# Graph convolutions' sums by row gathers in place of a stored adjacency

## The chip, the cores and the metric

The kernel runs on one core of a Trainium2 chip. The metric is the device time of one execution in microseconds (us); lower is better. The engines are named as in the profile: PE multiplies matrices (PEld is its weight load), DVE is the vector engine, ACT the scalar engine, POOL is GpSimd, and SP only issues DMAs. DMAs can be issued by SP, by ACT or by POOL; those whose rows are addressed by an index in memory (DMA_INDIRECT in the profile) are issued by POOL.

## The reference

There are N = 2500 nodes with D = 256 features, and E = 40000 edges sorted by their destination. The input passes through two blocks; each adds a graph convolution and a mixer to `x`, and then a set of expert networks.

```python
xn = _layernorm(x)
x = x + sage(xn, src, dst) + linear_mix(xn)      # mean over the neighbours, @ W_l.T, + xn @ W_r.T
x = x + top2_of_8_experts(_layernorm(x))
xn = _layernorm(x)
x = x + gcn(xn, src, dst) + transformer(xn)      # transformer: 4 layers, linear attention, FFN of 1024
x = x + experts(x)                               # gelu(x@W1), argmax gate of 8, prob * (H@Wd[e] + bd[e])
```

The change is in `gcn`, two graph convolutions with symmetric norms, where every node is also its own neighbour:

```python
src, dst = concat([src, loops]), concat([dst, loops])
deg = segment_sum(ones, dst); dis = rsqrt(deg)
norm = dis[src] * dis[dst]
h = segment_sum((x @ W1)[src] * norm[:, None], dst) + b1
h = where(h >= 0, h, alpha * h)
h = segment_sum((h @ W2)[src] * norm[:, None], dst) + b2
```

## The kernel before

The 2500 nodes stand as 20 tiles of P = 125 rows (NT = 20), in five groups of four tiles (NG = 5, GT = 4, GC = 500 columns). The code is a straight list of engine instructions: a scheduler orders each engine's queue and puts in the semaphores, so on one engine an instruction that waits holds back all that stand behind it. Work is interleaved by Python generators and by `between` callbacks, which set the order within an engine.

**First stage (0 to about 340 us).** The edge list becomes an adjacency matrix. `build_tile` makes one-hot rows of source and destination, multiplies them on PE (L722), and ACT copies the counts into a bf16 tile `edges` (L725), one group of 500 destinations at a time, each with all 20 source tiles. `neighbours` (L284; its matmul is L292) sums the neighbours' rows as matmuls: for each source tile three bf16 terms of the fp32 table times the counts, in two halves of the features. Its `between` builds the next group's `edges` and moves on the gating of the last group. Then `aT<-pa` copies (L750) take the sums from PSUM, two adds put the products into `X` (L762, L763), and the group's gating scatters its rows, sorted by expert, to `sorted` in DRAM (L407, on POOL). For the second block's use, identity is added to the diagonal blocks (L753) and each group's `edges` is stored as `adj` in DRAM, 12.5 MB in all.

**Second block (628 to about 1815 us).** `first_norm` normalizes the rows and calls `conv_in` for each group: `xn @ W1` times `dis`, kept as three bf16 terms in `table` (`split3`, ACT and POOL) and stored as `tab1` for a general path. `attention(l)` runs the four transformer layers; within one, `ffn` (L1148) works through the groups. `conv_1(g)`, the first convolution of a group, reads that group's `adj` back in pieces and calls `neighbours` again (`pa<-piece,table`); groups 0 and 1 run in layer 0, then one in each layer:

```python
            for g in range(NG):
                if max(g - 1, 0) == l:
                    conv_1(g)
```

It multiplies by `dis` along the columns (`along_rows`), adds b1, applies the two-sided ReLU with `alpha`, multiplies by W2 (`conv_in` again) and stores the terms as `terms2`. `conv_2()` stands behind the fourth layer: it loads `terms2`, calls `neighbours` for five groups (`mm<-piece,table`), turns the sums and adds them, times `dval`, to `X` (L972). GpSimd has two large adds in `ffn`: b2 into `Y` (L1151) and, in the last layer, `Y` into `X` (L1171), and it issues the loads of `b2` and `gm` at the start of each layer (L1029, L1031).

**Last stage.** From 1815 us the gates sort the rows by expert, and from 1960 us the experts work on blocks of 128 rows, each gathered by its index (L1345, POOL) and scattered to the output (L1403, POOL).

A general path, in a loop that runs only if the fast path's tables do not hold the edges (`lost`), follows each block.

Of the kernel before, what the change touches and what calls it, by code (L numbers as in the profile page):

```python
# [9 lines left out]
F32 = mybir.dt.float32  # L10
I32 = mybir.dt.int32
# [5 lines left out]
N = 2500  # L17
# [15 lines left out]
KC = 2  # L33
# [17 lines left out]
def gps_kernel(ctx: ExitStack, tc: tile.TileContext, a, out):  # L51
# [69 lines left out]
    ones = const.tile([P, 128], F32, name="ones")  # L121
    V.memset(ones, 1.0)
# [11 lines left out]
    adj = dram.tile([NG, P, NT, GC], BF16, name="adj")  # L134
    kth = scan.tile([128, 128], BF16, name="kth")
    G.iota(kth, pattern=[[1, 128]], base=0, channel_multiplier=0, allow_small_or_imprecise_dtypes=True)
    identb = scan.tile([P, P], BF16, name="identb")
    V.tensor_copy(identb, ident[:P, :P])
# [24 lines left out]
    begin = probe.tile([P, NQ], I32, name="begin")  # L163
# [47 lines left out]
    cnt = const.tile([P, NT], F32, name="cnt")  # L211

    def count_edges(pool):
# [15 lines left out]
        counts = dram.tile([N], F32, name="counts")  # L229
        nc.sync.dma_start(counts.rearrange("(q m n) -> m q n", q=NQ, n=BD), per)  # L230
        byrow = pool.tile([NT, P], F32, name="byrow")
        nc.sync.dma_start(byrow, counts.rearrange("(i p) -> i p", p=P))
        pc = psum2.tile([P, NT], F32, tag="cx", name="pc")
        T.transpose(pc, byrow, ident[:NT, :NT])
        V.tensor_copy(cnt, pc)
        return lost

    def gather_sums(pool, acc, table):
# [6 lines left out]
        gh = pool.tile([128, CH], F32, name="gh")  # L245
        V.tensor_scalar(gh, ge[:, :, 1], 1.0 / P, -0.496, ALU.mult, ALU.add)
        V.tensor_scalar(gh, gh, MAGIC, -MAGIC, ALU.add, ALU.add)
        gf = pool.tile([128, CH], F32, name="gf")
        V.tensor_copy(gf, ge[:, :, 1])
        V.scalar_tensor_tensor(gf, gh, -float(P), gf, ALU.mult, ALU.add)  # L250
        gs = pool.tile([128, CH], I32, name="gs")
        V.scalar_tensor_tensor(gs, gf, float(NT), gh, ALU.mult, ALU.add)
# [20 lines left out]
    def along_rows(pool, v, g):  # L273

        ps = psum2.tile([128, GC], F32, tag="ag", name="ps")
        for k in range(GT):
            dg = pool.tile([P, P], F32, tag="dg", name="dg")
            V.tensor_scalar(dg, ident[:P, :P], v[:, g * GT + k:g * GT + k + 1], None, ALU.mult)
            T.matmul(ps[:, k * P:(k + 1) * P], ones, dg, start=True, stop=True)
        row = pool.tile([128, GC], F32, tag="row", name="row")  # L280
        S.copy(row, ps)
        return row

    def neighbours(g, table, piece, between=None, banks=None):  # L284


        pa = banks or [psum2.tile([128, GC], F32, tag="ag", name=f"pa{c}") for c in range(2)]
        for k in range(NT):
            e = piece(k)
            for c in range(2):  # L290
                for n in range(3):
                    T.matmul(pa[c], table[:, k, n, c * 128:(c + 1) * 128], e,  # L292
                             start=(k == 0 and n == 0), stop=(k == NT - 1 and n == 2))
            if between is not None:
                between(k)
        return pa
# [238 lines left out]

    sorted1 = adj.rearrange("g p k d -> (g p k d)").bitcast(F32)[0:NE // 2 * N * RW].rearrange("(r c) -> r c", c=RW)
# [75 lines left out]
    with tc.tile_pool(name="lay0", bufs=1) as lay0:  # L612
# [91 lines left out]
        degrees(cnt)  # L704
# [5 lines left out]
        with tc.tile_pool(name="build", bufs=1) as build:  # L710
# [15 lines left out]

            ahead = new_edges()
            for k in range(GT):
                build_tile(ahead, 0, k)
            for g in range(NG):  # L730
                edges = ahead
                for lo, hi in ((0, g * GT), ((g + 1) * GT, NT)):
                    if hi > lo:
                        move(nc.sync, adj[g][:, lo:hi, :], edges[:, lo:hi, :])
# [5 lines left out]
                def between(k):  # L740

                    if k % GT == 1 and k < GT * GT and g + 1 < NG:
                        build_tile(ahead, g + 1, k // GT)
                    if gating is not None and k in (7, 15):
                        next(gating)

                pa = neighbours(g, xb, lambda k: edges[:, k, :], between)
# [3 lines left out]
                for k in range(GT):  # L751
                    o = edges[:, g * GT + k, k * P:(k + 1) * P]
                    V.tensor_tensor(o, o, identb, ALU.add)  # L753
                move(nc.sync, adj[g][:, g * GT:(g + 1) * GT, :], edges[:, g * GT:(g + 1) * GT, :])
# [23 lines left out]
    with tc.tile_pool(name="lost0", bufs=1) as pool, tc.For_i(0, n_lost, 1):  # L778
# [8 lines left out]
        nc.sync.dma_start(tab0.rearrange("(p k) d -> p k d", p=P), acc[:, :, :D])  # L787
# [78 lines left out]
    with tc.tile_pool(name="big", bufs=4) as big, tc.tile_pool(name="hid", bufs=8) as hid, \  # L866
# [30 lines left out]
        tab1 = dram.tile([N, D], F32, name="tab1")  # L897
        terms2 = dram.tile([NG, P, GT, 3, D], BF16, name="terms2")
        table = conv.tile([P, NT, 3, D], BF16, name="table")
        dval = const.tile([P, NT], F32, name="dval")  # L900
        V.tensor_scalar(dval, dis, valid, None, ALU.mult)

        def conv_in(g, src, w, keep):

            for b in range(0, GT, 2):
                i = g * GT + b
                if keep and b:
                    t = conv.tile([P, 3, D], F32, tag="t3", name="t3")[:, 0:2, :]
                else:
                    t = conv.tile([P, 2, D], F32, tag="t", name="t")  # L910
                ps = psum2.tile([P, 2, D], F32, tag="ag", name="ps")
                for k in range(2):
                    for c in range(2):
                        T.matmul(ps[:, k, :], src[:, c, (b + k) * P:(b + k + 1) * P], w[:, c, :], start=(c == 0), stop=(c == 1))
                V.tensor_tensor(t, ps, dis[:, i:i + 2, None].to_broadcast([P, 2, D]), ALU.mult)
                if keep:
                    move(nc.sync, tab1.rearrange("(p k) d -> p k d", p=P)[:, i:i + 2, :], t)
                    split3(table[:, i:i + 2], t, G)
                else:
                    t3 = conv.tile([P, 2, 3, D], BF16, tag="t3", name="t3")  # L920
                    split3(t3, t, G)
                    move(nc.sync, terms2[g][:, b:b + 2], t3)

        def conv_1(g):


            def piece(k):
                if k % KC == 0:
                    piece.tile = conv.tile([P, KC, GC], BF16, tag="piece", name="piece", bufs=4)
                    move(nc.sync, piece.tile, adj[g][:, k:k + KC, :])  # L930
                return piece.tile[:, k % KC, :]

            row = along_rows(conv, dis, g)
            pa = neighbours(g, table, piece)
            u = conv.tile([128, 2, GC], F32, tag="u", name="u")
            for c in range(2):
                V.tensor_tensor(u[:, c, :], pa[c], row, ALU.mult)
            for c in range(2):
                neg = conv.tile([128, GC], F32, tag="row", name="neg")
                V.tensor_scalar(neg, u[:, c, :], bcol[:, 0, c:c + 1], 0.0, ALU.add, ALU.min)  # L940
                S.activation(u[:, c, :], u[:, c, :], AF.Relu, bias=bcol[:, 0, c:c + 1])
                V.scalar_tensor_tensor(u[:, c, :], neg, alpha, u[:, c, :], ALU.mult, ALU.add)
            conv_in(g, u, wc2, False)

        def conv_2():

            for g in range(NG):
                move(nc.sync, table[:, g * GT:(g + 1) * GT], terms2[g])
            u = big_T()

            def sums(g):
                def piece(k):
                    if k % KC == 0:
                        piece.tile = hid.tile([128, GC], F32, tag="h", name="piece")[:P].bitcast(BF16).rearrange(
# [534 lines left out]
```

## Time and profile before

| | us |
|---|---|
| median of three runs | 2159.9 (2159.02 to 2162.81) |
| the profiled execution | 2163.04 |
| its span | 2161.2, mean granted PE clock 0.96 |

The stages of the profiled execution, from its busy time in stretches:

| stretch, us | what runs | PE busy | DVE busy | POOL busy |
|---|---|---|---|---|
| 0 to 340 | edges, first convolution, gating | 252.5 | 207.1 | 87.0 |
| 340 to 570 | first experts | 186.2 | 74.5 | 47.6 |
| 570 to 628 | `first_norm` | 50.1 | 42.5 | 18.4 |
| 628 to 1678 | four layers and `conv_1` | 1044.5 | 447.6 | 89.6 |
| 1678 to 1815 | `conv_2` | 133.2 | 27.0 | 2.5 |
| 1815 to 1960 | gates and sorting | 122.6 | 31.5 | 23.9 |
| 1960 to 2161 | experts | 170.9 | 65.9 | 46.5 |

The page's slices show how evenly PE is filled, and the clock it was granted, each digit a tenth in a slice of 54 us:

```profile
PE   2699973999689999999999999999999998995996
...
POOL 2302322222130201001010010000211000122222
PEclk9799986999799999999999999999999999997999
```

A row of groups in the profile reads: line, engine, operation, written tile `<-` read tiles, shapes, count, then busy time and mean ns of one, then the idle time of the engine just before and what ended it. A row that answers for one line gives the least, median and greatest duration in ns, and the first and last start.

### The profile page before, as it was taken

The numbers are of one execution on the slowest core, as the hardware profiler recorded it, in microseconds if no ns is written. First come the engines' busy times: TensorE is split into PE (matmuls) and PEld (weight loads), VectorE is DVE, ScalarE is ACT, GpSimd is POOL, SyncE is SP. The second block draws the span as 40 slices with busy tenths as digits, with TensorE's granted clock in tenths as the row PEclk, the third lists the DMA queues.
The fourth block names the chain that finished last, engine by engine and source line by source line (L and its number), as shares of the span: only waits on it lengthen the run. The fifth ranks groups of instructions, "written<-read, shape, count | busy, mean of one in ns | idle before, by whom it ended". The sixth has DMA issues, their size and how long they took to land. (4 is left out here: it accounts for less than half of the span.)

```text
span 2161.2 us, 25307 instructions
## 1 busy us (share of the span) xinstructions
PE 1959.8 (91%) x9035; PEld 1309.3 (61%) x9035; DVE 896.2 (41%) x2822; ACT 580.8 (27%) x989; POOL 315.6 (15%) x288
## 2 busy tenths in 40 slices
PE   2699973999689999999999999999999998995996
PEld 2556643887466577676676767666676443334665
DVE  6866542333644346435463443635441023212333
ACT  1433201222361222223323133232322000331220
POOL 2302322222130201001010010000211000122222
PEclk9799986999799999999999999999999999997999
DMA  4022445665512200111001100022100435111100
GB/s 121 9 81 71 110 144 165 200 198 175 139 39 66 70 6 13 35 43 38 0 13 42 50 24 0 13 63 77 29 0 1 126 95 183 36 28 33 33 19 24
DMA packets 83119, 141.30 MB, mean 65 GB/s; under 512 B 18700, under 2 KB 64254, under 8 KB 82227
## 3 DMA queue, kind: packets, MB, share of 16 engines
q1 hardware_dynamic: 66193, 112.35, 17.7%
q0 software_dynamic: 13840, 20.89, 3.5%
q10 hardware_dynamic: 2949, 6.33, 1.1%
q8 instruction: 76, 1.25, 0.2%
q14 instruction: 61, 0.49, 0.1%
HBM read 103.85 MB, written 37.61 MB: 65 GB/s over the span
## 5 line engine op out<-in xcount | busy, mean ns | idle before, releaser
L1166 PE MATMUL mm<-w,h 128*125 128x256 f32 x1280 | 286.1, 379 | 0.0
L1156 PE MATMUL mm<-xT,w 128*128 128x500 f32 x640 | 282.9, 582 | 0.0
L1166 PEld LDWEIGHTS mm<-w,h 128*125 128x125 f32 x1280 | 239.2, 188 | 43.0 <-issue 9.2
L292 PEld LDWEIGHTS <-table 125*128 125x128 bf16 x1200 | 117.1, 98 | 126.7 <-issue 1.7
L1156 PEld LDWEIGHTS mm<-xT,w 128*128 128x128 f32 x640 | 119.0, 190 | 109.2 <-issue 100.8
L1159 ACT ACTIVATE h<-mm,bf 128x500 f32<-128x500 f32 x160 | 107.6, 677 | 216.6 <-PE mm L1156 216.5
L1151 POOL TENSOR_TENSOR tok<-tok,b 125x1024 f32<-125x1024 f32 x20 | 47.3, 2364 | 684.5 <-DVE tok L1143 632.4
L292 PE MATMUL pa<-piece,table 125*128 125x500 bf16 x600 | 138.1, 374 | 0.0
L292 PE MATMUL pa<-edges,xb 125*128 125x500 bf16 x600 | 134.4, 377 | 1.7 <-ACT edges L725 1.7
L292 PE MATMUL mm<-piece,table 125*128 125x500 bf16 x600 | 127.3, 374 | 0.0
L1167 DVE TENSOR_TENSOR tok<-tok,mm 125x256 f32<-125x256 f32 x80 | 33.5, 419 | 206.8 <-PE mm L1166 178.7
L1394 PE MATMUL py<-wd,taken 128*128 x432 | 96.9, 381 | 10.0 <-DVE taken L1384 10.0
L828 PE MATMUL mm<-xc,wt 128*128 128x128 f32 x752 | 97.1, 283 | 7.6 <-DVE idx L834 4.0
L828 PEld LDWEIGHTS mm<-xc,wt 128*128 128x128 f32 x752 | 89.6, 194 | 18.0 <-DVE xc L824 12.9
L292 PEld LDWEIGHTS <-xb 125*128 125x128 bf16 x600 | 58.2, 100 | 64.0 <-issue 4.1
L842 PE MATMUL py<-w,h 128*128 x376 | 96.1, 382 | 0.9 <-ACT h L832 0.9
L1394 PEld LDWEIGHTS py<-wd,taken 128*128 128x128 f32 x432 | 81.2, 190 | 25.3 <-DVE taken L1384 13.1
L832 ACT ACTIVATE h<-mm,wt 128x128 f32<-128x128 f32 x188 | 53.8, 369 | 137.6 <-issue 127.3
L357 ACT ACTIVATE xT<-mm,mixc 128x500 f32<-128x500 f32 x80 | 58.9, 768 | 116.1 <-PE mm L352 82.0
L725 ACT CAST edges<-mm 125x500 bf16<-125x500 f32 x100 | 64.7, 784 | 89.4 <-PE mm L722 80.3
L1254 PE MATMUL mm<-xTf,w 128*128 128x500 f32 x160 | 79.2, 618 | 6.0 <-DMA w<-in_L_ffn_W_dram 6.0
L1067 PE MATMUL mm<-xT,wa 128*128 128x500 f32 x160 | 76.4, 622 | 3.9 <-ACT xT L357 3.9
(363 smaller groups left out, 2833.6 us busy)
## 6 DMA issues: line engine op xcount, KB each, us to landing
wt<-in_expert_in_dram SPq DMA_DIRECT2D x47, 514.0 KB
piece<-adj SPq DMA_DIRECT2D x100, 218.8 KB
w<-in_L_mix_W_dram SPq DMA_DIRECT2D x8, 1024.0 KB
wd<-in_L_ffn_Wd_dram SPq DMA_DIRECT2D x8, 1024.0 KB
xs<-sorted SPq DMA_DIRECT2D x47, 130.0 KB
w<-in_L_ffn_W_dram SPq DMA_DIRECT2D x8, 512.0 KB
adj<-edges SPq DMA_DIRECT2D x2, 1750.0 KB
terms<-t SPq DMA_DIRECT2D x10, 336.0 KB
```

Source lines behind the costliest of these rows:

```text
L292: T.matmul(pa[c], table[:, k, n, c * 128:(c + 1) * 128], e, start=(k == 0 and n == 0), stop=(k == NT - 1 and n == 2))
L357: S.activation(o, ps, AF.Identity, bias=shift[:, c:c + 1], scale=gain[:, c:c + 1])
L725: S.copy(o.rearrange("p s (n d) -> p n s d", d=BD), ps[:P].rearrange("p (n s d) -> p n s d", n=BD, d=BD))
L828: T.matmul(ps[:, j * TS:(j + 1) * TS], wt[:, c * F0 + j * 128:c * F0 + (j + 1) * 128], xc[:, c * TS:(c + 1) * TS], start=(c == 0), stop=(c ...
L832: S.activation(h[:, j * TS:(j + 1) * TS], ps[:, j * TS:(j + 1) * TS], AF.Gelu, bias=wt[:, 2 * F0 + j:2 * F0 + j + 1])
L842: T.matmul(ps, h[:, j * TS:(j + 1) * TS], w2[:, ds(e, 1), j, :], start=(j == 0), stop=(j == NJ - 1))
L1067: T.matmul(ps, wk[:, kc, c * 128:(c + 1) * 128], hT[:, kc, g * GC:(g + 1) * GC], start=(kc == 0), stop=(kc == 1))
L1156: T.matmul(ps, w1[:, c, j * 128:(j + 1) * 128], fT[:, c, g * GC:(g + 1) * GC], start=(c == 0), stop=(c == 1))
L1159: S.activation(h, ps, AF.Gelu, bias=bf[:, l, j:j + 1])
L1166: T.matmul(ps, hh[j][:, k * P:(k + 1) * P], w2[:, j, :], start=(j == 0), stop=(j == nj - 1))
L1254: T.matmul(ps, w1[:, c, j * 128:(j + 1) * 128], xT[:, c, g * GC:(g + 1) * GC], start=(c == 0), stop=(c == 1))
L1394: T.matmul(ps, h[:, j * TS:(j + 1) * TS], wd[:, ds(e, 1), j, :], start=(j == 0), stop=(j == nj - 1))
```

## The change

The adjacency is built for the first block only and no longer stored. In its place each node gets a rank by its number of edges (`rank_nodes`): a one-hot of the count in 64 bins, running sums by ten matmuls, and a record of 16 bytes (node, first edge, `dis`) scattered to its rank in `byrank`. That table is read back as 20 columns of 128 ranks; for each, one gather fetches a window of as many edges as the list `MOST` allows its ranks, and edges that belong to another node are replaced by row N, a row of zeros. The steps of `rank_nodes` run within the first stage, from `between` of groups 1 to 4.

A convolution is then, for each of the 20 columns of ranks, one gather of the nodes' own rows and up to 42 of neighbours' rows, each of 128 rows of 1 KB, four to a tile, summed by DVE. The first convolution's sums get b1 and the ReLU in rank order and are scattered to `tab2`; the second's are scattered to `sums2`, and `conv_out` multiplies by `dval` and W2 and adds to `X` behind the last layer. `conv_step` puts the sums' DVE instructions at places within the layers, by a calendar of constants. `sorted1`, which used the memory of `adj`, has its own tile and is filled with zeros in the first stage.

Besides that, the `b2` and `gm` loads go from POOL's queue to ACT's, the two GpSimd adds go to DVE, tables in DRAM are laid out by node, and the general path gets a flag of its own (`lost1`).

```diff
+MOST = (42, 24, 22, 21, 20, 19, 18, 18, 17, 16, 16, 15, 15, 14, 14, 13, 13, 12, 11, 9)
+SUM = 4
+LEAD = 5
+GATHER = 1.27
+LANDING = 12.0
+LAYER = 237.0
+AHEAD = 40.0
+NBIN = 64
...
+    def rank_nodes(pool):
...
+        for i in range(NT):
+            made.append(G.indirect_dma_start(
+                out=byrank, out_offset=bass.IndirectOffsetOnAxis(ap=at[:, i:i + 1], axis=0), in_=rec[:, i, :], in_offset=None,
+            ))
...
+        yield
+        byr = pool.tile([128, NT, 4], F32, name="byr")
+        nc.gpsimd.dma_start(byr, byrank.rearrange("(j p) c -> p j c", p=128))
...
+        yield
+        wins = pool.tile([128, heads_of[NT], 2], I32, name="wins")
+        hit = pool.tile([128, heads_of[NT]], F32, name="hit")
+        for j in range(NT):
+            part = slice(heads_of[j], heads_of[j + 1])
+            G.indirect_dma_start(
+                out=wins[:, part, :].rearrange("p e t -> p (e t)"), out_offset=None, in_=pairs,
+                in_offset=bass.IndirectOffsetOnAxis(ap=from_[:, j:j + 1], axis=0),
+            )
+            V.tensor_scalar(hit[:, part], wins[:, part, 0], byr[:, j, 0:1], None, ALU.is_equal)
+        yield
...
+            for n in range(0, 80, 16):
+                nc.sync.dma_start(sorted1.rearrange("(p r) c -> p r c", p=P)[:, n:n + 16, :],
+                                  nothing[:, None, :].to_broadcast([P, 16, RW]))
...
-                        move(nc.sync, adj[g][:, lo:hi, :], edges[:, lo:hi, :])
...
+                    if g > 0 and k in (3, 11, 19):
+                        next(ranking, None)
...
-                for k in range(GT):
-                    o = edges[:, g * GT + k, k * P:(k + 1) * P]
-                    V.tensor_tensor(o, o, identb, ALU.add)
-                move(nc.sync, adj[g][:, g * GT:(g + 1) * GT, :], edges[:, g * GT:(g + 1) * GT, :])
...
-        def conv_1(g):
...
-        def conv_2():
...
+        def gathers(tab, finish):
...
+            steps = [(j, k) for j in range(NT) for k in range(0, MOST[j] + 1, SUM)]
+            pieces = {}
...
+            def fetch(n):
+                j, k = steps[n]
+                t = conv.tile([128, SUM, D], F32, tag="piece" if k else "total", name="piece", bufs=LEAD + 1 if k else 3)
+                m = min(SUM, MOST[j] + 1 - k)
+                for i in range(m):
+                    by = node[:, j:j + 1] if k + i == 0 else nbr[:, heads_of[j] + k + i - 1:heads_of[j] + k + i]
+                    G.indirect_dma_start(out=t[:, i, :], out_offset=None, in_=tab,
+                                         in_offset=bass.IndirectOffsetOnAxis(ap=by, axis=0))
+                pieces[n] = t, m
...
+            for n in range(LEAD):
+                fetch(n)
+            for n, (j, k) in enumerate(steps):
+                yield GATHER * (sum(min(SUM, MOST[i] + 1 - b) for i, b in steps[:n + 1]) + j)
+                t, m = pieces.pop(n)
+                if k == 0:
+                    total = t
                 else:
...
+                    V.tensor_tensor(total[:, :m, :], total[:, :m, :], t[:, :m, :], ALU.add)
+                if n + LEAD < len(steps):
+                    fetch(n + LEAD)
+                if k + SUM > MOST[j]:
+                    V.tensor_tensor(total[:, 0:2, :], total[:, 0:2, :], total[:, 2:4, :], ALU.add)
+                    sums = conv.tile([128, D], F32, tag="sums", name="sums", bufs=3)
+                    V.tensor_tensor(sums, total[:, 0, :], total[:, 1, :], ALU.add)
+                    finish(j, sums)
...
+        def between(j, o):
...
+            b = conv.tile([128, D], F32, tag="b", name="b")
+            S.activation(b, b1row, AF.Identity, scale=disr[:, 0, j:j + 1])
+            V.scalar_tensor_tensor(o, o, disr[:, 1, j:j + 1], b, ALU.mult, ALU.add)
+            neg = conv.tile([128, D], F32, tag="neg", name="neg")
+            V.tensor_scalar(neg, o, 0.0, alpha, ALU.min, ALU.mult)
+            V.scalar_tensor_tensor(o, o, 0.0, neg, ALU.max, ALU.add)
...
+            to_nodes(tabs[1], j, o)
...
+        def conv_step(now):
+            while under and under[0][1] + under[0][2] + LANDING <= now:
+                run, _, begun = under.pop(0)
+                with tc.issue_after(last["add"]):
+                    passed = next(run, None)
+                if passed is not None:
+                    under.insert(0, (run, passed, begun))
+                elif begun == 0:
+                    run = gathers(tabs[1], lambda j, o: to_nodes(sums2, j, o))
+                    under.append((run, next(run), now))
...
+        def conv_out(g, rows, turned):
...
+            s = rows[:, g * GT:(g + 1) * GT, :]
+            move(nc.gpsimd, s, by_node(sums2)[:, g * GT:(g + 1) * GT, :])
+            V.tensor_tensor(s, s, dval[:, g * GT:(g + 1) * GT, None].to_broadcast([P, GT, D]), ALU.mult)
+            sT = turned[:, :, g * GC:(g + 1) * GC]
+            transpose_group(turned, g, lambda k: s[:, k, :])
...
-                nc.gpsimd.dma_start(b2, row_bcast(a["L1_mix_b2"], l * D, D, 128))
+                nc.scalar.dma_start(b2, row_bcast(a["L1_mix_b2"], l * D, D, 128))
...
+                conv_step(LAYER * l + AHEAD * i / NT * 0.7)
...
-                G.tensor_tensor(o, o, b2[:P, None, :].to_broadcast([P, GT, D]), ALU.add)
+                V.tensor_tensor(o, o, b2[:P, None, :].to_broadcast([P, GT, D]), ALU.add)
...
+                def beside(step):
+                    conv_step(LAYER * l + AHEAD + (LAYER - 1.6 * AHEAD) * (g + step / (nj + GT)) / NG)
...
-            for g in range(NG):
-                if max(g - 1, 0) == l:
-                    conv_1(g)
...
-        conv_2()
+        with tc.issue_after(last["product"]), tc.issue_after(last["add"]):
+            conv_step(1e9)
+            rows, turned = big_tok(), big_T()
+            for g in range(NG):
+                conv_out(g, rows, turned)
```

## The prediction

> **What bounds the kernel now.** I read the page's forty slices first, then the costliest groups, then a table of busy time by stage.
>
> ```profile
> PE 1959.8 (91%) x9035; PEld 1309.3 (61%) x9035; DVE 896.2 (41%) x2822; ACT 580.8 (27%) x989; POOL 315.6 (15%) x288
> ...
> L1151 POOL TENSOR_TENSOR tok<-tok,b 125x1024 f32<-125x1024 f32 x20 | 47.3, 2364 | 684.5 <-DVE tok L1143 632.4
> L292 PE MATMUL pa<-piece,table 125*128 125x500 bf16 x600 | 138.1, 374 | 0.0
> ...
> L292 PE MATMUL mm<-piece,table 125*128 125x500 bf16 x600 | 127.3, 374 | 0.0
> ```
>
> PE is the bound and POOL nearly idle. The two L292 groups are the graph convolutions. By stage (columns: window, length, busy us of PE, PEld, DVE, ACT, POOL, PE clock, DMA share, GB/s):
>
> ```profile
> 300.00:340.00 40.00, 11.85 (x53) 9.92 (x51) 14.55 (x60) 1.52 (x2) 16.47 (x16) 0.60 0.74 214
> ...
> 628.00:897.00 269.00, 265.99 (x1141) 180.99 (x1142) 114.43 (x359) 69.34 (x106) 27.49 (x20) 1.00 0.13 35
> 897.00:1156.00 259.00, 258.11 (x1084) 177.28 (x1083) 117.84 (x385) 78.41 (x115) 18.18 (x12) 1.00 0.10 27
> 1156.00:1417.00 261.00, 260.11 (x1094) 178.96 (x1093) 117.87 (x385) 78.41 (x115) 18.19 (x12) 1.00 0.10 27
> 1417.00:1678.00 261.00, 260.12 (x1093) 178.77 (x1091) 97.49 (x282) 78.41 (x115) 25.77 (x13) 1.00 0.12 33
> 1678.00:1815.00 137.00, 133.15 (x649) 64.19 (x648) 27.02 (x102) 3.46 (x6) 2.51 (x2) 0.99 0.35 97
> ```
>
> Rows two to five are the four transformer layers, PE over 98% busy; the last is the second convolution with nothing beside it. In the timeline its last `X` add ends at 1811.6 and the gates' first matmul (L1254) starts at 1819.5, after 6.0 us on its weights. Without convolution a layer needs about 229 us of PE (259 less 28.3 of L292 and about 2 of its small products; the first 209).
>
> **What goes.** All of both L292 groups: some 30 us in each of three layers, 60 in the first, and the 137 us stage. The stored adjacency (12.5 MB) and its readings go too, but the new zero-fill of `sorted1` writes 10.4 MB in the same stage, so I count nothing for bandwidth. GpSimd's 25 large adds move to VectorE. The bound then passes to POOL.
>
> **What comes: gathers.** The sum of `MOST` is 349, plus 20 own rows: 369 gathers (the short description says 367) and 20 scatters per convolution, 778 POOL instructions for two. The nearest row is the expert stage's gather of 128 rows of 1040 bytes; this rate is the forecast's main term.
>
> ```profile
> L1345 POOL DMA_INDIRECT X<-adj,whence x20: 945/956/1131, 1965.7 to 2066.2; - x20
> ```
>
> In the timeline one follows another after 0.30 us of issue, so the period is 1.26 us (1967.06, 1968.33, 1969.58). A gather lands 2.9 us after its start. 389 × 1.26 = **490 us per convolution**, 980 for both: more than the four layers' PE work of 209 + 3 × 229 = 896. DMA itself is no limit: four gathers in 1965 to 1990 took 7.9% of the sixteen engines over 25 us, 0.5 us each.
>
> **A rule that speaks against it.** The Trainium skill's page "SBUF — State Buffer", box "The 'DVE blocks DMA' trap", says that while VectorE runs a two-port operation (an fp32 copy in SBUF), GpSimd is locked out and cannot write its DMA's descriptors: 620 ns became about 3100. Its section "Who interferes with whom" exempts a tensor_tensor, thus the new adds, but not tensor_scalar. The trace has POOL DMAs beside such operations (start, length, engine; "x2" is two operations in one row):
>
> ```profile
> 1969.58 0.95 POOL L1345 DMA_INDIRECT X<-adj,whence  x1 [0.30 <-issue]
> 1969.58 0.74 DVE L1357 TENSOR_SCALAR xh<-X 128x256 f32<-128x256 f32 x2 [3.07 <-DMA X<-adj,whence]
> ...
> 2145.59 0.69 DVE L1384 COPY taken<-hs 128x1024 f32 x1
> 2145.62 1.50 POOL L1403 DMA_INDIRECT out_dram<-yo,idx  x1 [4.02 <-DVE yo L1402]
> ```
>
> The scatter took 1.50 in place of 0.97, 0.53 more: something like the lock is there. But of nine gathers that had 0.41 us tensor_scalars beside them, as the first, eight took 0.95 and one 1.13: +0.02 on average. In the layers there are 140 such tensor_scalars (L1143, L365). By the trace's worst case or the rule's "blocked until the VectorE operation ends" that is 140 × 0.5 = +70 us; at 3.1 us per gather it would be ruin. By the nearest row it is 3 us. I take +5 and keep 0 to 70.
>
> **What comes: VectorE.** A row of 125x256 costs 0.42 us (L1167), 125x512 0.69 (L1109), hence about 1.23 for 1024 elements (estimate). Per convolution 80 adds, at most 98 us, and 20 folds of 0.69 + 0.42 = 22; conv 1's finish 20 × 3 × 0.45 = 27; the moved adds 25 × 1.23 = 31. That is +298 us, less about 30 removed: 448 becomes 716 us, 77% of some 930. VectorE stays below full, but it is in order: an add put before a softmax operation delays what PE waits for by up to 1.23 us, and an add whose gather hasn't landed stops all behind it. The diff places adds by a calendar of 1.27 us per gather and 237 us per layer, with 12 us for landing; so adds normally find data. In the built order 16 adds lie behind the last layer's last `Y` add. Bounds: nothing (POOL is later anyway) to the case below; I take +5.
>
> **What comes: ranking, in the first stage.** Some sixty small VectorE operations (about 22 us) and ten matmuls fit in gaps: VectorE is 60% busy there. The POOL chain doesn't fit. In the built order VectorE does the last ranking sum after group 2's `X` adds (236 us); then POOL: 20 scatters at 1.49 (L407's 125 rows: 1.19 + 0.30) = 30, to 266, landed 269; the load of `byr` in 2,560 pieces of 16 bytes, which no row shows: from 0.64 (a plain POOL load, L1031) to 19 (2,560 at the gather's 0.95/128), I take 10, landed 282; 20 gathers at 1.26 = 25, to 307, landed 310. The 20 `hit` operations wait for these, and in VectorE's order they stand **ahead of group 3's `aT<-pa` copy**, which ran at 262.4. Behind it are that group's `X` adds and gating. PE has only some 24 of group 4's 120 matmuls to put in between. POOL's order also puts the row scatters of groups 2 to 4 behind the chain. So aT is 48 us late; group 4's is about 43 late, and part of the old 29 us between it and its row scatters (11.6 were a wait for earlier scatters) goes. I take **+38** for everything from there on; bounds 10 (short load, slack in gating) and 60.
>
> **The small rest.** POOL's `b2` and `gm` loads go to ACT's queue: their buffers wait for the old reader in both versions, and a layer hides them; 0, if exposed at most 3 us for each of four layers. Two value loads: under 2 us.
>
> **Sum, on the profiled execution** (span 2161.2, 2163.0 with what lies around it). `tab1` is complete at 629.6 now, 667.6 with the late first stage. Conv 1: +490 = 1157.6. Turnaround: landing 2.9, adds and finish 3.7, scatter 1.3, its landing 3 = 11, to 1168.6. Conv 2: 1658.6; its last sum stored 1670. conv_out: ten POOL loads of 500 rows a group at 7.4 ns a row, about 22 us, 3 of landing, 4.5 for the last group's product and adds = 30, to 1700. The old 7.9 to L1254: 1708, against 1819.5, or −111.5. With +5 collisions, +5 VectorE order and +3 because PE sits idle for about 100 us before the gates (300 to 340 shows clock 0.60 in such a gap): **−98, 2065**. The profiled execution lies 3 us above the runs' median of 2159.9, so I forecast 2062.
>
> **The rivals.**
> - A, the ranking chain is hidden (+10 in place of +38): the gap in 300 to 340 speaks for it, VectorE's order against. 2062 − 28 = 2034, and 2015 if the tail is short too.
> - B, VectorE sets the layers: 185 inserted operations, half of each 1.23 us felt by PE, would be +114 us, layers of 257; I take 245. Layers end at 667.6 + 980 = 1648; the 16 late adds bring 63 gathers and 7 scatters, less a lead of 20: 50 × 1.26 = 63 us; then 11 + 30 + 8 = 1760, 59.5 before 1819.5, or 2103 − 3 = 2100 in the runs. PE's 98% speaks for it, 23% free VectorE against.
> - C, slower: the gather's period itself rises beside a VectorE that is 77% busy, because descriptor writing is locked out, as in the 1.50 us scatter. It decides from 98 / 778 = 0.126 us, a period of 1.39. At 1.50: 778 × 0.24 = +187, so 2065 + 187 − 3 = 2249. For it: the 1.50, the skill's box, and that the old layers show hardly any POOL DMA. Against: L407 kept 1.19 (at most 1.28) in 100 to 300, where VectorE was 60% busy.
> - D, the list doesn't hold the input's degrees and the general loop also runs: hundreds of us more. Counted from the reference's input, the largest degrees by rank block are 32, 23, 21 ... 9, all within `MOST`.
>
> **Chances.** Forecast 0.45 (own range 2035 to 2085), A 0.14, B 0.20, C 0.18, D 0.03. The range 2000 to 2175 takes in A and B whole and C's mild end. About 0.2% is what a measurement can tell from no change; only a strip between B and C falls there, 0.02. Faster 0.78, slower 0.20.
>
> **What would show it.** Gathers 1.26 us apart and POOL over 90% busy from about 668 to 1670 (C: more than 1.39); the last `hit` near 310 and group 3's aT right behind it; layer starts 230 to 240 us apart (B: over 245); PE empty for some 100 us before L1254's successor near 1720. I am wrong if VectorE's waits on gathers within the layers come to tens of us, since then PE also waits, or if the `byr` load is dear.

## The result: slower by 1.2%

The changed kernel took 2186.6 us (2183.1 to 2193.4) against 2161.4 (2159.0 to 2166.7) for the kernel before on the same chip: a ratio of 1.0117, interval 1.0086 to 1.0148. The prediction was 2062, faster by 98 us, and its range ended at 2175. The profiled execution has a span of 2191.7 us, 30.5 more than before. First the page: line 1, the slices, and the two new groups.

```profile
PE 1747.0 (80%) x7817; PEld 1216.7 (56%) x7817; DVE 1118.3 (51%) x3160; ACT 557.6 (25%) x954; POOL 1067.6 (49%) x1045
...
PE   2699935699868799978998799987899206994997
...
POOL 2301653122205767676777277776677771022222
...
L1024 POOL DMA_INDIRECT piece<-tab,nbr x698 | 728.6, 1044 | 259.9 <-issue 188.3
...
L1036 DVE TENSOR_TENSOR piece<-piece 128x1024 f32<-128x1024 f32 (+3 forms) x160 | 176.9, 1113 | 108.8 <-DMA piece<-tab,nbr 105.1
```

PE lost 213 us of busy time and the kernel none. POOL is seven tenths busy in the layers' slices (its 0.30 us of issue before each gather are not counted), and one slice in their middle shows 2: something keeps it waiting. The mean gather takes 1044 ns, not 950. The slices with 2 and 0 on PE are the tail, in which PE waits for the sums.

The table of stages, cut at the keys' maxima that begin each layer's context, at the last `Y` add and at the first matmul of the gates. First before, then after:

```profile
624.00:923.00 299.00, 294.40 (x1258) 197.33 (x1257) 127.97 (x399) 85.19 (x128) 28.65 (x21) 1.00 0.13 36
923.00:1183.00 260.00, 259.11 (x1089) 178.20 (x1088) 117.70 (x385) 78.28 (x115) 18.18 (x12) 1.00 0.10 27
1183.00:1443.00 260.00, 259.11 (x1089) 178.25 (x1088) 117.36 (x385) 78.41 (x115) 18.19 (x12) 1.00 0.10 27
1443.00:1678.00 235.00, 234.13 (x987) 164.16 (x985) 86.18 (x248) 66.64 (x96) 25.77 (x13) 1.00 0.12 32
1678.00:1819.00 141.00, 133.15 (x649) 64.19 (x648) 31.02 (x123) 3.46 (x6) 2.51 (x2) 0.98 0.37 104
```

```profile
663.00:931.00 268.00, 241.72 (x958) 170.56 (x956) 161.42 (x442) 76.15 (x114) 188.44 (x186) 0.96 0.42 107
931.00:1194.00 263.00, 237.56 (x944) 167.44 (x944) 172.51 (x470) 79.30 (x120) 193.16 (x181) 0.96 0.35 104
1194.00:1466.00 272.00, 241.79 (x944) 169.47 (x944) 163.33 (x442) 75.49 (x112) 180.40 (x172) 0.95 0.39 96
1466.00:1712.00 246.00, 218.49 (x856) 157.30 (x856) 137.61 (x302) 62.23 (x89) 177.88 (x169) 0.93 0.32 94
1712.00:1852.00 140.00, 25.70 (x129) 21.10 (x128) 55.19 (x148) 3.46 (x6) 80.45 (x82) 0.61 0.36 102
```

Read the second column downwards. What lies ahead of the layers grew from 624 to 663 us: **+39**. The layers went from 1054 to 1049 us: **−5**, although PE has 107 us less to do in them. The stretch from the last `Y` add to the gates went from 141 to 140: **−1**; the 137 us of the second convolution on PE became 100 us of waiting for the remaining gathers and 40 of `conv_out`. What follows took 2 us less. The sum is the 31 us of the result. All that was freed on PE was filled again, and the ranking stayed as net cost.

### The profile page after: what moved, and what is told of

Its sections match the earlier page's. It is cut to its first block, busy times and chain, and to the rows that moved or that the text cites. A ratio compares the mean times of both kernels' runs of the same rounds, so it can differ in the third digit from the quotient of the medians.

```text
span 2191.7 us, 24023 instructions
## 1 busy us (share of the span) xinstructions
PE 1747.0 (80%) x7817; PEld 1216.7 (56%) x7817; DVE 1118.3 (51%) x3160; ACT 557.6 (25%) x954; POOL 1067.6 (49%) x1045
## 5 line engine op out<-in xcount | busy, mean ns | idle before, releaser
L1024 POOL DMA_INDIRECT piece<-tab,nbr x698 | 728.6, 1044 | 259.9 <-issue 188.3
L1278 PE MATMUL mm<-xT,w 128*128 128x500 f32 x640 | 287.5, 591 | 0.9 <-ACT xT L443 0.9
L1036 DVE TENSOR_TENSOR piece<-piece 128x1024 f32<-128x1024 f32 (+3 forms) x160 | 176.9, 1113 | 108.8 <-DMA piece<-tab,nbr 105.1
L438 PE MATMUL mm<-ident,tok 125*128 125x125 f32 x360 | 54.6, 293 | 173.4 <-DVE tok L1086 107.3
L438 PEld LDWEIGHTS mm<-ident,tok 125*128 125x128 f32 x360 | 44.4, 150 | 188.9 <-DVE tok L1086 107.7
L935 POOL DMA_INDIRECT back<-yo,idx x47 | 45.7, 973 | 166.9 <-DVE idx L921 100.7
L493 POOL DMA_INDIRECT sorted<-rows,to x40 | 49.1, 1227 | 149.0 <-DVE to L488 126.3
L1212 PE MATMUL pk<-kt,tok 125*128 125x256 f32 x320 | 90.5, 438 | 16.4 <-DVE kt L102 15.0
L1528 POOL DMA_INDIRECT out_dram<-yo,idx x27 | 27.1, 1002 | 135.5 <-DVE yo L1527 117.2
L1251 DVE TENSOR_TENSOR tok<-tok,po 125x256 f32<-125x256 f32 x80 | 30.2, 415 | 121.8 <-PE po L1248 121.4
```

The lines of the kernel that those rows point to most:

```text
L438: T.transpose(ps[:, k * P:(k + 1) * P], src_of(k)[:, c * 128:(c + 1) * 128], ident[:P, :P])
L493: moved.append(G.indirect_dma_start(out=table, out_offset=bass.IndirectOffsetOnAxis(ap=to[:, k:k + 1], axis=0), in_=rows[:, k, :], in_offs ...
L1024: G.indirect_dma_start(out=t[:, i, :], out_offset=None, in_=tab, in_offset=bass.IndirectOffsetOnAxis(ap=by, axis=0))
L1036: V.tensor_tensor(total[:, :m, :], total[:, :m, :], t[:, :m, :], ALU.add)
L1212: T.matmul(pk[c], rows[:, i, c * 128:(c + 1) * 128], kt, start=(i == 0), stop=(i == NT - 1))
L1278: T.matmul(ps, w1[:, c, j * 128:(j + 1) * 128], fT[:, c, g * GC:(g + 1) * GC], start=(c == 0), stop=(c == 1))
```

## The experiments

Some of the runs can't be read for their time: e5, e7 and e8; e9 to e11; r5 and r6. In these three groups, every kernel with gathers took 2429 to 2532 us, while the kernel before, run between them, took its usual 2161 to 2163; three of the very same programs gave 2151, 2154 and 2158 in another group. It isn't the chip alone: r5 and r6 ran on the one on which e4 had taken 2187. The section on the hardware shows what was seen in them; in the table they are set apart. Kernels without gathers were not touched (e6 2068, and r4, the same program, 2065).

| run | what differs from the changed kernel | us | ratio to before, interval |
|---|---|---|---|
| r1 | nothing | 2186.8 | 1.0118 (1.0101 to 1.0135) |
| e4 | ranking early, hits behind aT | 2186.7 | 1.0125 (1.0108 to 1.0142) |
| r2 | ranking split, all its waits behind aT | 2151.4 | 0.9960 (0.9946 to 0.9974) |
| r3 | `LAYER` 262 | 2154.1 | 0.9967 (0.9957 to 0.9976) |
| r7 | total in PSUM | 2158.5 | 0.9989 (0.9981 to 0.9996) |
| e1 | sums by tensor_reduce | 2233.1 | 1.0334 (1.0316 to 1.0351) |
| e3 | no gathers | 2089.4 | 0.9663 (0.9647 to 0.9679) |
| r4 | no gathers, adds or finish | 2065.2 | 0.9551 (0.9536 to 0.9567) |
| e2 | no adds and folds | 2393.5 | 1.1069 (1.1050 to 1.1087) |
| apart | e5 (r2's kernel), e7 (r3's), e8, e9 (r7's), e10, e11, r5, r6 | 2429 to 2532 | not used |

### e1: sums by tensor_reduce

```diff
...
-                    V.tensor_tensor(total[:, :m, :], total[:, :m, :], t[:, :m, :], ALU.add)
...
+                V.tensor_reduce(parts[:, k // SUM, :], t[:, :m, :].rearrange("p m d -> p d m"), AX.X, ALU.add)
```

> The pieces of four rows, and then the pieces' sums of a rank block, are added by tensor_reduce, which reads one operand, in place of tensor_tensor adds with two operands in SBUF; everything else as in the changed kernel. Theory A (a gather that starts while VectorE runs a tensor_tensor with two SBUF inputs waits for its end; 116 of the 117 gathers over 1.1 us start so): the gathers' mean falls from 1.044 to at most 0.975 us, gathers over 1.1 us from 117 to under 45, and, if POOL's chain sets the end, the time falls by 30 to 60 us, to about 2130 to 2155. Theory B (any VectorE work locks POOL out, or the calendar alone sets the pace): mean gather still over 1.02, or the mean falls and the time stays within 10 us of 2187.

The first half came: the mean gather fell to 0.973 us, and 33 took over 1.1. The time did not: +46. The row of the reduction in this run tells why (least, median, greatest ns):

```profile
L1035 DVE TENSOR_REDUCE parts<-piece x200: 397/1907/1957, 673.1 to 1844.3; 128x256 f32<-128x1024 f32 x94, 128x256 f32<-128x768 f32 x4, 128x256 f32<-128x256 f32 x2
```

It takes 1.9 us for what the add did in 1.2, VectorE gained 208 us of work, and POOL's waits for it grew from 47 to over 130 us. So e1's time is no test of what collisions cost; r7's is.

### e2 and e3: adds without gathers, gathers without adds

e2 leaves out L1036 and L1040, e3 the gathers.

> Leaves out the adds of pieces to the total (L1036) and the fold of four rows to two (L1040), so the sums hold only two gathered rows; all 738 gathers, 40 scatters and the finishing operations stay. If the adds are what stretches the convolutions (collisions 76 us, POOL waiting for adds 84 us, layers slowed by adds in VectorE's queue): gathers at 0.95 to 0.97, both convolutions from first gather to last scatter in 980 to 1000 us in place of 1140, a layer in 230 to 240 us in place of 257, time about 2040 to 2055. If the gathers' own traffic or their descriptor writing slows the layers: a layer stays at 250 or more and the time above 2100.

> Leaves out all 738 gathers; the adds run at their places on two tiles of zeros that are always there, the scatters stay. If VectorE's order makes the layers long (an inserted add delays what PE waits for): a layer stays at 240 to 257 us and the time is about 2040 to 2090, the layers ending near 1640 to 1690. If the layers are long because VectorE waits for gathers that are late (36 us within the layers in the profile) or because gathers hold VectorE's operations: a layer takes 228 to 236 us and the time is about 2000 to 2025.

e2 left its question open; only the mean gather, 0.967 us, came as expected. Without adds POOL is no longer held back and runs far ahead; the scatter of a rank block's sum stands behind many gathers in POOL's queue, and VectorE, with three `sums` buffers, waited for it (160 us on scatters, 192 on gathers, in ten waits). e3's layers took 260, 260, 259 and 236 us, 1015 in all, as the first of its two alternatives had it: nearly the length they have with the gathers (1049), so the gathers' share of the layers' length is about 34 us.

### e6 and r4: the bare layers

```diff
...
-                    V.tensor_tensor(sums, total[:, 0, :], total[:, 1, :], ALU.add)
-                    finish(j, sums)
+                    finish(j, still[0][:, 0, :])
```

Gathers, adds and the finish operations are gone; 40 scatters of zeros remain. Twenty of them wait for nothing and ran among the first experts (391 to 468 us), and the layers began at 694 us in place of 663, so only the layers of these runs are compared, not their whole time.

> Leaves out the gathers, the adds and folds, and the first convolution's finish; only the 40 scatters of a tile of zeros, and conv_out, are left of the convolutions. It gives the layers' length with nothing beside them. If the inserted adds make the layers long (260 us without gathers, against 230 that PE's own work takes): 228 to 236 us a layer. If the old convolution's matmuls hid VectorE's delays, and the layers can't run at PE's pace without them (or the moved adds and DMAs cost it): 245 us or more.

> The bare layers again (no gathers, adds or finish), now beside kernels of one machine. The first look had 253, 256, 256 and 231 us a layer, with PE busy 235.6 of 256. The same is expected: 250 to 257 for the middle layers, against 260 before with the first convolution inside, so that the convolution's matmuls had cost a layer only 4 to 8 us, not 30; or 228 to 236 if the first look was disturbed.

Stages of this run, two middle layers:

```profile
946.00:1202.00 256.00, 235.48 (x944) 166.45 (x944) 116.06 (x379) 74.52 (x109) 0.00 (x0) 0.97 0.05 14
1202.00:1458.00 256.00, 235.59 (x944) 166.59 (x944) 115.98 (x379) 74.31 (x109) 0.00 (x0) 0.97 0.05 14
```

With nothing beside it a layer takes 256 us, and PE is idle for 20 of them. It waits for VectorE's normalized rows, for the keys' exponentials and for the queries' softmax (7.3, 6.3 and 2.9 us in the second layer); before, its waits in the same layer came to 0.5 us. The two longest waits of r4, and what PE did at the same two places in the kernel before:

```profile
950.90 1.22 PE L1195 MATMUL mm<-ident,xT 128*125 128x128 f32 x4 [5.16 <-ACT xT L1186]
...
1005.79 1.97 PE L438 MATMUL mm<-ident,tok 125*128 125x125 f32 x8 [7.28 <-DVE tok L1250]
```

```profile
922.80 5.23 PE L292 MATMUL pa<-piece,table 125*128 125x500 bf16 x24
...
973.54 6.92 PE L292 MATMUL pa<-piece,table 125*128 125x500 bf16 x32
```

**The first convolution's matmuls had run in time in which PE would otherwise wait.** The large adds that the change moved to VectorE are still in r4, but they don't make these waits: the second layer's first one starts at 1006.64, behind the 7.28 us. The other 6.5 us between 229 and 256 are busy time: in the second layer the `pk` products take 418 ns on average in place of 388 and the keys' transposes 310 in place of 275, at a granted clock of 0.97 in place of 1.00; whether the clock or the waits lengthen them is not separated. The old layer with its convolution took 260. So taking it off PE was worth 4 us a middle layer, where I had counted 30, and 60 us in the four (1054 to 994), where I had counted 150. From bare (994) the adds bring 21 us (e3, 1015) and the gathers 34 (1049).

### e4, e5 and r2: the ranking

e4 starts the ranking one group earlier and holds `hit` behind group 3's aT copy; e5 and r2 (one program) also hold `from_` and `whose` behind an aT copy:

```diff
-                    if g > 0 and k in (3, 11, 19):
+                    if k in (3, 11, 19):
...
+            with tc.issue_after(rank_nodes.late):
+                V.tensor_scalar(hit[:, part], wins[:, part, 0], byr[:, j, 0:1], None, ALU.is_equal)
...
+                    if c == 0:
+                        rank_nodes.late = made.ins
```

> The ranking starts one group earlier and its twenty hit operations are kept behind group 3's aT copy; the convolutions are as in the changed kernel. If the ranking chain ahead of aT costs the first stage 38 us: the first gather of the first convolution starts 30 to 42 us earlier (near 632 in place of 671) and the time falls by 25 to 42 us, to 2145 to 2162. If the first stage is late for another reason (the zero-fill's or the weights' DMAs), the first gather stays after 655.

> As the run that started the ranking early, but every VectorE operation that waits for the ranking chain now stands behind an aT copy: from_ behind group 2's, hit and whose behind group 3's (in the run before, from_ and whose stood ahead of group 2's and 3's and waited 24 and 22 us). If these waits ahead of aT make the first stage late: PE's wait for aT falls from 41 to under 12 us, the first gather starts near 632 to 645 and the time falls by 20 to 38 us, to 2148 to 2167. If the stage is late for another reason: the first gather stays after 655 and the time within 8 us of 2187.

> The rank split again. If its long layers came with the machine: 2145 to 2167, 20 to 38 us less than the changed kernel beside it (the first gather starts about 25 us earlier). If they come with the edit: about 2460.

e4 didn't change the time, and its own row says why: PE still waited 40.6 us for aT. In the built order `from_` (24.0 us for the `byr` load) and `whose` (22.0 us for the windows) had come to stand ahead of group 2's and 3's copies, so the stall had moved by one group. In r2 none stands there. PE's waits in the first stage, the changed kernel and then r2 (us in total, times, longest):

```profile
PE mm L848 <- DVE aT L841: 37.7, 1, 37.7
PE px L909 <- DMA b<-in_L_mix_b_dram: 32.2, 1, 32.2
```

```profile
PE px L919 <- DMA gm<-in_L_mix_bo_dram: 32.1, 1, 32.1
PE mm L446 <- DVE tok L1140: 16.3, 1, 16.3
```

The wait for aT is gone (the 32 us wait of the next stage is there in both), the first gather starts at 633 in place of 667, and the time falls by 35 us. The layers' table would start at 627, against 659 in r1 and 624 before: what VectorE waited for ahead of aT is nearly all of the ranking's cost.

### r1, e7, e8 and r3: the calendar

```diff
-LAYER = 237.0
+LAYER = 262.0
```

> The changed kernel itself, beside the next two. In the runs of the rank split and of the two calendars, layers took about 350 us and every engine but POOL stood still for 76 to 145 us of them, without a wait that the trace names, although the rank split changes nothing in the layers. If that comes with the edits (their place in the instruction stream): 2180 to 2195 here as before, and the next two near 2460 again. If it comes with the machine on which they ran: all three move together; the changed kernel then lies near 2450, or the next two come down to 2120 to 2190.

> LAYER 262 in place of 237, the length that the layers really have; 158 of the 160 adds now lie ahead of the last Y add, in place of 144. If the tail of 100 us behind the last layer is there because the calendar is late: the end of the sums moves from 100 to at most 40 us behind the last Y add, with layers at most 10 us longer in all, and the time falls by 40 to 70 us, to 2115 to 2150. If POOL's rate (1.25 us and collisions) sets the end: VectorE waits for gathers within the layers instead, these grow by what the tail loses, and the time stays within 15 us of 2187.

> LAYER 262 and GATHER 1.36 (a gather with its collisions: 1.045 + 0.30), so adds stand where gathers really are; 150 of 160 adds ahead of the last Y add. If VectorE's waits for late gathers cost the layers: waits on gathers within the layers under 15 us (36 before), tail 40 to 70 us, time 2130 to 2165. If POOL sets the end: within 15 us of 2187.

> The calendar with LAYER 262 again. If its long layers came with the machine: 40 to 70 us less than the changed kernel beside it if the tail is the calendar's fault; within 15 us of it if POOL's rate sets the end. If they come with the edit: about 2460.

r1 gave 2186.8 and r3 2154.1, so the long layers of e5 and e7 were not the edits'. (e8, which also sets `GATHER` to 1.36, ran only in a group that is set apart.) In r3 the last scatter of sums starts 16 us behind the last `Y` add in place of 95, but the layers grew from 1047 us to 1095. Both sides of my alternative came in part: the tail shrank by 79 us and the layers gave back 48. Within the layers VectorE waited 91 us for gathers, in place of 34:

```profile
DVE piece L1036 <- DMA piece<-tab,nbr: 91.0, 25, 7.4
```

So an add that stands late makes POOL wait, and one that stands early makes VectorE, and behind it PE, wait.

### e9 and r7: the total in PSUM

```diff
-                    total = t
-                else:
-                    V.tensor_tensor(total[:, :m, :], total[:, :m, :], t[:, :m, :], ALU.add)
+                    total = [psum2.tile([128, 2, D], F32, tag="ag", name=f"total{h}") for h in range(2)]
...
+                    if k == 0:
+                        S.copy(total[h], t[:, 2 * h:2 * h + 2, :])
+                    elif w > 0:
+                        V.tensor_tensor(total[h][:, :w, :], total[h][:, :w, :], t[:, 2 * h:2 * h + w, :], ALU.add)
```

> The total of a rank block lies in two PSUM tiles, so an add reads one operand from SBUF (a piece of 512 elements, two adds of about 0.69 us in place of one of 1.22); the first piece and one half are copied by ScalarE. If a gather waits for tensor_tensor operations with two SBUF inputs: gathers over 1.1 us fall from 106 to under 45, POOL's excess over 0.95 us from 71 to under 30. If these collisions set the end, the time falls by 30 to 45, to 2140 to 2157; if the calendar does (16 adds behind the last Y add, which need about 60 us of gathers after it), by at most 20.

> The total in PSUM alone, again, since its first look fell on a machine on which every kernel with gathers was some 300 us longer. On a machine without that: gathers over 1.1 us under 45 in place of 106. If the gathers' collisions (71 to 76 us of POOL's time) set the end of the changed kernel: 2140 to 2157. If the late calendar does, since 16 adds with about 60 us of gathers lie behind the last Y add: at most 20 us below 2187, and POOL's waits for adds grow by what the collisions lose. Near 2500 nothing follows.

The timeline of the changed kernel shows what is at stake (start, length):

```profile
1078.86 1.22 DVE L1036 TENSOR_TENSOR piece<-piece 128x1024 f32<-128x1024 f32 x1
1079.24 1.65 POOL L1024 DMA_INDIRECT piece<-tab,nbr  x1 [0.31 <-issue]
1081.20 0.95 POOL L1024 DMA_INDIRECT piece<-tab,node  x1 [0.30 <-issue]
...
1084.37 1.22 DVE L1036 TENSOR_TENSOR piece<-piece 128x1024 f32<-128x1024 f32 x1
1084.94 1.46 POOL L1024 DMA_INDIRECT piece<-tab,nbr  x1 [0.30 <-issue]
```

The add ends at 1080.08; the gather that started inside it ends 0.81 us later. The second pair has 0.81 too. Of the 117 POOL DMAs over 1.1 us in the changed kernel, 116 start while a tensor_tensor or scalar_tensor_tensor with two SBUF operands runs (three of them up to 0.02 us ahead of its start), and nearly all end about 0.8 us after it; the gathers that start elsewhere take 0.954 on average. In r7, where one operand of the adds lies in PSUM, the gathers over 1.1 us fall from 106 (r1) to 34. Of 73 that start with over 0.3 us of such an add left none is longer; of those that stay long, 16 start in a moved `b2` add, which still has two SBUF operands.

```profile
L1024 POOL DMA_INDIRECT piece<-tab,nbr x698 | 677.7, 971 | 279.6 <-issue 181.3
```

POOL's excess over 0.95 us falls from 70 to 19 us, and the time by 28 us, between the two sides of my alternative. The rest came back as waits: POOL's waits longer than its normal issue grew from 96 to 121 us in all, those for adds from 45 to 57. That the collisions are real and that this edit is worth 28 us is shown. The edit also gives ScalarE two kinds of copies and changes when a piece's buffer comes free, which was not tested apart; that the calendar takes back the other half fits the waits.

### e10, e11, r5 and r6: all together

e10 joins the rank split with `LAYER` 262, e11 adds the PSUM total; r5 and r6 are the same programs again.

> The rank split and LAYER 262 together. The rank split alone gave 2151, the calendar alone 2154, against 2187. If they are independent: 2115 to 2125.

> All three: total in PSUM, rank split, LAYER 262. If POOL's rate sets the end once the calendar is right, it is 30 to 60 us below the run without the PSUM total, 2060 to 2090; layers come down from 280 to about 265, since VectorE waits less for gathers. If the collisions only fill time that POOL would wait for adds anyway: within 12 us of it.

> The rank split and LAYER 262 without the PSUM total, beside it. If the two are independent: 2115 to 2125. If the machine is as in the first look: near 2430, and nothing follows from either.

> The total in PSUM, rank split and LAYER 262 again, since its first look fell on a machine on which every kernel with gathers ran some 300 us longer, with engines standing still at no named wait, while the kernel before did not. On a machine without that: 2060 to 2090 if the gathers' collisions set the end once the calendar is right; 2105 to 2130, as the two without PSUM would give if independent (2151 and 2154 from 2187), if they only fill time that POOL waits for adds. Gathers over 1.1 us under 40 in any case.

All four runs are among those set apart (2429 and 2499, then 2452 and 2532). What the edits give together was not measured. Of what was, r2, r3 and r7 beat both kernels: 0.4%, 0.3% and 0.1% below the kernel before.

## Why the prediction was wrong

**Right: the first stage.** +38 was predicted, +39 measured. The last `hit` ran at 306 us (310 predicted), group 3's aT copy at 307; r2 takes this away. That the sum came so close is in part luck: the `byr` load took 1.4 us and landed 4.1 us after its issue, where I took 10 and 3, while the ranks' scatters had landed 6 us later than I said (275 in place of 269).

**Right: the gather's base rate.** 0.946 us median and 0.30 of issue: 1.25 a piece, 972 us for 778, against 980.

**Right: the tail's own work.** From the landed sums (1812) to the gates' first matmul (1852) took 40 us, against 38 predicted. The 3 us for a PE that had been idle did not show: what follows took 2 us less than before.

**The step that failed: the convolutions' length.** I had 1002 us from the complete `tab1` to the stored sums; it was 1142 (670 to 1812). POOL's 1140 us from the first gather to the last scatter divide into 778 × 0.95 = 739 of base, 230 of normal issue, 75 of gathers made longer, and 96 of longer waits. In the sum the last two were "+5 collisions" and "+5 VectorE order", with 11 for the turnaround. My own sign of being wrong came too: VectorE waited 36 us for gathers within the layers.

- *Collisions.* I sized them by the only rows I had, tensor_scalars beside gathers, and took the Trainium skill's exemption of tensor_tensor for the adds ("SBUF — State Buffer", section "Who interferes with whom"). The same section says that a VectorE instruction with two SBUF inputs contends with a GpSimd instruction that reads SBUF; that a gather's row indices lie in SBUF, I overlooked. The page reports a probe in which tensor_tensor did not stall a DMA, and marks its reason as inferred; for these gathers the measurement decides against it. That the reading of the indices is the reason, no run here shows. The tensor_scalars that I had sized cost nothing: of 20 gathers that start with over 0.3 us of an fp32 tensor_scalar of the normalization left, none is over 1.1 us. The collisions took 75 us of POOL's time; avoiding most of them (r7) gave 28 of the whole.
- *VectorE's order.* I took the layers' pace from PE's work, 229 us, and the 237 of the calendar for granted. Layers took 262 on average. Most of that isn't the adds: the bare layers take 256 in the middle. With a calendar of 237 in layers of 262, adds come later than their gathers, POOL waits with its pieces ready, and 16 adds with their gathers fall behind the last layer. The 33 us of r3 measure this, net of what the layers give back.
- *What was removed.* "Without convolution a layer needs about 229 us of PE" was busy time read as length. PE's 98% hid that the convolution's matmuls were what kept it busy; the waits that they had filled are the 20 us of r4.
- *The turnaround.* A third of POOL's longer waits is one wait, which I had left out. From the last gather of the first convolution to the first of the second it took 42 us, where I had 11:

```profile
1260.49 0.97 POOL L1046 DMA_INDIRECT tab<-sums,node  x1 [31.55 <-DVE y L392]
1263.02 1.98 POOL L1024 DMA_INDIRECT piece<-tab,node  x1 [1.57 <-DMA tab<-sums,node]
```

The last rows had landed at 1223.7, but the add that takes them ran at 1254.6: between a layer's keys and its feed-forward groups the calendar has no place for an add, in each layer of this profile for 39 to 43 us, and the turnaround fell into that gap. In r3 it took 24.

**The rivals.** C named this mechanism, a longer period beside a busy VectorE, with a limit of 1.39 us; the measured period over both convolutions, all waits included, is 1140 / 778 = 1.47, or 1.41 without the turnaround. Its cause was half right: longer gathers make 0.10 us of the 1.47, waits 0.12, and it is tensor_tensors that lengthen them. B had the layers at 245 with a tail of 63 us; they were 262, with 100. B and C came together, and I had counted each alone. A did not come, since the first stage grew by 39.

## What to carry to other kernels

Before taking work off a full engine, ask what its neighbours in the queue would wait for without it: a stage that is left is as long as the busy time that remains and the waits that the work had filled, and one run with the work simply left out (here 256 us in place of 229) settles it. An order of instructions fixed by a calendar is only as good as the pace it assumes; where the pace comes out 10% slower, one side waits for the other throughout; look also for stretches in which it offers no place at all. When many small indexed DMAs run beside VectorE, count the collisions as rows of the timeline, and try one operand of VectorE's long operations in PSUM, which gave 28 us here.

## What the runs showed of the hardware

- An indexed DMA of GpSimd (0.946 us) that starts early in a VectorE tensor_tensor with two SBUF operands ends about 0.8 us after it: it takes up to 2.0 us beside an add of 1.22 (two of 778 took longer). Beside adds with one operand in PSUM (73 in r7) or a tensor_reduce of the pieces (over 170 in e1) none took over 1.1 us.
- A tensor_reduce that adds four rows of 256 with a stride of 1 KB takes 1.907 us (e1); the tensor_tensor over the same 1024 elements 1.218.
- Programs with gathers can be about 300 us longer on some occasions: e7 took 2461 us and r3, the same program, 2154. In e7's layers PE, VectorE and ScalarE stood still together for 152 us in 22 stretches of over 2 us (26 us in 7 in r3), in most of which POOL went on with gathers of 0.95 us; r5's layers show 26 such stretches of 178 us. One of e7's, seen from ScalarE and PE:

```profile
689.62 1.65 PE L1212 MATMUL pk<-kt,tok 125*128 125x256 f32 x4 [2.34 <-issue]
...
691.06 1.48 PE L1207 MATMUL mm<-ident,xT 128*125 128x128 f32 x6
...
712.29 0.37 ACT L100 COPY kt<-mm 125x256 f32<-125x256 f32 x1 [26.94 <-issue]
```

The copy's input was complete at 692.5 and it ran at 712.3, with no wait named. What holds the engines then was not found; it stays open.
